# Two state-space layers and a convolution tail on one core: Softplus in one function, sums of two tiles together, a second product tile on GpSimd, and a new slot table

## The chip, the core and the metric

The kernel runs on one core of a Trainium2 chip, in float32 throughout. The metric is the device time of one execution in microseconds (us). The kernel before takes 7343.06 us, the median of three runs (7335.37 to 7346.82). The profiled execution has a span of 7346.1 us.

## What is computed

Four layers follow one another on an input of 8 images, 384 channels, 32 by 32 pixels, so 1024 tokens per image. Layers 0 and 1 each hold a Mamba block (768 inner channels, 16 states per channel), layer 1 also a channel gate and an MLP (384 to 1536 to 384). Layers 2 and 3 are 13 by 13 depthwise convolutions with a 1 by 1 convolution between. The change touches the Mamba blocks, whose core is:

```python
u = silu(conv(x_in) + conv_b)
dt_lo, Bm, Cm = split(u @ x_proj_w.T)                # 24, 16 and 16 columns
delta = softplus(dt_lo @ dt_proj_w.T + dt_proj_b)
h = h * exp(delta * A) + delta * u * Bm              # for every token in turn, 768 channels x 16 states
y = sum over states of h * Cm, + u * D
out = (y * silu(z)) @ out_proj_w.T
```

## The kernel before, in words

**Units, blocks, items.** A unit is one layer, one image and one half of its tokens (512 of 1024), so there are 32 units. A unit has six blocks `d` of 128 channels, and a block has eight items `n`. An item holds 64 of the channels (`h` says which 64) and four of the 16 states (`g` says which four): a tile of 128 partitions by two rows of 512 tokens. That makes 1536 items. Before, `h, g = divmod(n, 4)`: four items of one `h` follow each other, then four of the other.

**What one item costs.** Its steps are on four engines:

- `decay` (L528, ScalarE): two `Exp` activations write the factor of the recurrence into the PSUM tile `h`, of which there are two.
- `inflow` (L535, GpSimd): the product `dbu` of `B` and the repeated `delta * u`; four buffers.
- `scan` (L545 for the first half of an image in one instruction, L549 for the second half in two instructions): VectorE runs the recurrence, then multiplies by `C` into a tile `hc` (L554), of which there are three.
- `keep` (L562, ScalarE, first halves only) stores the last state.
- `fold` (L577, TensorE): two products with 32 output columns each sum the states into a quarter of the PSUM tile `acc` each. With `n == 0` the skip product (L573) opens `acc`, and `y_out` (L580, VectorE) takes it away.

For the items in `AT["pool"]`, before only `n == 1`, the multiplication by `C` is done by GpSimd instead (L564, in place), one slot later.

**The step sizes.** For each block, softplus is made of parts: a product into PSUM (L474), then on ScalarE `Abs`, `Relu` and `Exp` (L479 to L481), an `Identity` and a `Ln` (L486, L487), one more `Identity` (L490), and on GpSimd three tile operations that put the result together (L491, L494, L497). A fourth (L502) multiplies by `u`, and a small one (L504, first halves) separates the rows in the scan. `delta` and its product with `u` go to DRAM (`flat`, L508) and come back repeated over the states (`repeat`, L517): two tiles for each of the two, each filled by four transfers.

**The order of work.** There is no automatic scheduling: every engine's queue is the program order that a slot plan writes out by hand. Slot `K` belongs to item `K`. The main loop emits for each slot: `keep` of item K-1, `decay` of item K+1, `inflow` of item K+2, `scan` of item K, `fold` of item K-1, and then everything that the plan has put in this slot. The plan places the projections of the *next* unit (`x`, `z`, `ranks`), its layer norm, the convolution, the batches of `Silu`, the output product of the *last* unit and the MLP of finished images, all by the slot numbers in the table `AT`. Engines work in order, so a waiting instruction holds up all that its queue has behind it.

**Tables of ScalarE.** `Exp` and `Ln` share a table set. `Silu` and the MLP's `Gelu` are in others. So `table` (L446) does a batch of them and then loads the set with `Exp` again (`exp_ln`, L305). Before, each unit has four batches of `Silu` and each MLP four of `Gelu`.

**The end.** After slot 1536 the rest of the plan runs in slot order without scans: here the output products and the MLPs of the last images. Then come the two depthwise passes (L947) and the pointwise product (L981).

Of the kernel before, what the change touches and what calls it, by code (L numbers as in the profile page):

```python
# [16 lines left out]
P = 128  # L17
# [82 lines left out]
class Unit:  # L100


    def __init__(self, layer, b, half):
        self.layer, self.b, self.half = layer, b, half
        self.cols = slice(half * T, (half + 1) * T)
        self.us, self.zs, self.ps, self.acc = [None] * KD, [None] * KD, {}, {}
        self.dr, self.ur, self.o, self.B, self.C, self.w = {}, {}, {}, {}, {}, {}

# [111 lines left out]
AT = {'in_ahead': 2, 'out_ahead': 2, 'taps_ahead': 3, 'norm': (-5, -2, -1, 0, 1, 2, 3, 3, 4, 5, 7, 12, 12, 12, 12), 'x': (13, 16, 18, 24, 26, 29), 'shift': 1, 'conv': 4, 'u': 5, 'silu': ((31, 3, 0), (34, 6, 1), (40, 6, 4), (58, 6, 6)), 'hid': 2, 'ranks': (33, 34, 35), 'z': (31, 35, 37, 39, 40, 41), 'B': (41, 44, 45, 46), 'C': (41, 42, 46, 48), 'step': (3, 4, 5, 6, 6, 7, 7), 'repeat': (13, 13, 15, 15), 'out': (0, 3, 8), 'out_half': 2, 'out_add': 3, 'out_gate': 0, 'res_ahead': 1, 'heads': 14, 'softmax': (16, 18, 19), 'attend': (19, 22, 25, 23), 'context': 29, 'hidden': (30, 31, 32, 34, 36, 38), 'gates': (42, 40, 46), 'mlp': 22, 'mlp_norm': (-6, 1, 2, 2, 3, 4, 5, 5, 5, 5, 7, 9, 9, 11, 11), 'mlp_plan': ((3, 60, 12, (23, 33, 42, 69)), (2, 44, 8, (22, 30, 38, 42)), (2, 44, 7, (18, 28, 40, 44))), 'fold0': (-18, -10), 'fold0_step': (3, 3), 'shifted': 2, 'flat': (9, 9), 'bc_out': 37, 'store': 2, 'mlp_gap': -2, 'px_ahead': 1, 'pool': (1,), 'prepare': (-40, 4),  # L220
# [3 lines left out]
def layers(tc, k, a, vec, x0, x1, x2, x3, lasting, got):  # L224
# [16 lines left out]
    with ExitStack() as st:  # L241
# [87 lines left out]
        def load_dt(s, d):  # L329
            s.w["dt", d] = work.tile([R + 1, P], F32, tag="w_dt", name="w_dt")  # L330
            nc.sync.dma_start(s.w["dt", d], s.layer.w["dt"][:, d * P : (d + 1) * P])
# [116 lines left out]

        def ranks(s, ds):

            if ds[0] == 0:
                s.xps = mm()
            for d in ds:
                nc.tensor.matmul(s.xps[:NX], s.w["xp"][:, d], s.us[d], start=d == 0, stop=d == KD - 1)
# [9 lines left out]
        def spread(s, key, g):  # L464

            t = work.tile([P, T], F32, tag=key, name=key, bufs={"B": 5, "C": 6}[key])
            at = ("BC".index(key) * NS + 4 * g) * T
            nc.sync.dma_start(t, bass.AP(s.bc.tensor, s.bc.offset + at, [[T, 4], [0, 32], [1, T]]))
            getattr(s, key)[g] = t


        def sp_in(s, d):
            s.sp = mm()
            nc.tensor.matmul(s.sp, s.w.pop(("dt", d)), s.dbc[: R + 1], start=True, stop=True)  # L474

        def sp_exp(s, d):
            s.e = work.tile([P, T], F32, tag="sp_e", name="sp_e", bufs=1)
            s.delta = work.tile([P, T], F32, tag="delta", name="delta", bufs=1)
            nc.scalar.activation(s.e, s.sp, AF.Abs)  # L479
            nc.scalar.activation(s.delta, s.sp, AF.Relu)  # L480
            nc.scalar.activation(s.e, s.e, AF.Exp, scale=-1.0)  # L481

        def sp_ln(s, d):
            s.one = work.tile([P, T], F32, tag="sp_w", name="sp_w", bufs=1)
            s.ln = work.tile([P, T], F32, tag="sp_l", name="sp_l", bufs=1)
            nc.scalar.activation(s.one, s.e, AF.Identity, bias=k["one"])  # L486
            nc.scalar.activation(s.ln, s.e, AF.Ln, bias=k["one"])  # L487

        def sp_one(s, d):
            nc.scalar.activation(s.one, s.one, AF.Identity, bias=k["minus"])  # L490
            nc.gpsimd.tensor_tensor(s.one, s.one, s.e, ALU.subtract)  # L491

        def sp_back(s, d):
            nc.gpsimd.tensor_tensor(s.ln, s.ln, s.one, ALU.subtract)  # L494

        def sp_delta(s, d):
            nc.gpsimd.tensor_tensor(s.delta, s.delta, s.ln, ALU.add)  # L497

        def sp_du(s, d):

            s.du = work.tile([P, T], F32, tag="sp_w", name="sp_w", bufs=1)
            nc.gpsimd.tensor_tensor(s.du, s.delta, s.us[d], ALU.mult)  # L502
            if s.half == 0:
                nc.gpsimd.tensor_tensor(s.delta[:, 0:1], s.delta[:, 0:1], far, ALU.add)  # L504

        def flat(s, d, which):
            got = dram.tile([P, T], F32, tag="dd" if which == "d" else "uu", name="dd" if which == "d" else "uu")
            nc.sync.dma_start(got, s.delta if which == "d" else s.du)  # L508
            (s.dr if which == "d" else s.ur)[d] = got, {}

        def repeat(s, d, which, h):

            dd, got = (s.dr if which == "d" else s.ur)[d]
            got[h] = work.tile([P, 2, T], F32, tag=f"r{which}", name=f"r{which}", bufs=2)
            for q in range(4):
                quarters = bass.AP(dd.tensor, dd.offset + 64 * h * T, [[T, 32], [32 * T, 2], [1, T]])
                nc.sync.dma_start(got[h][32 * q : 32 * q + 32], quarters)  # L517
# [4 lines left out]
        def decay(item):  # L522
            s, d, n = item
            h, g = divmod(n, 4)
            y = ps_h.tile([P, 2, T], F32, tag="h", name="h")
            for q in range(2):
                at = (d * 4 + 2 * h + q) * 4 + g
                nc.scalar.activation(y[:, q], s.dr[d][1][h][:, q], AF.Exp, scale=s.layer.A[:, at : at + 1])  # L528
            ready[item, "h"] = y

        def inflow(item):
            s, d, n = item
            h, g = divmod(n, 4)
            dbu = work.tile([P, 2, T], F32, tag="dbu", name="dbu", bufs=4)
            nc.gpsimd.tensor_tensor(dbu, s.B[g].unsqueeze(1).to_broadcast([P, 2, T]), s.ur[d][1][h], ALU.mult)  # L535
            ready[item, "dbu"] = dbu

        def scan(item):
            s, d, n = item
            h, g = divmod(n, 4)  # L540
            y, dbu = ready.pop((item, "h")), ready.pop((item, "dbu"))
            to = dbu if n in AT["pool"] else y
            if s.half == 0:
                flat_to, flat_y, flat_b = (t.rearrange("p q t -> p (q t)") for t in (to, y, dbu))
                nc.vector.tensor_tensor_scan(flat_to, flat_y, flat_b, 0.0, ALU.mult, ALU.add)  # L545
            else:
                for q in range(2):
                    first = state[:, d, 2 * h + q, g : g + 1]
                    nc.vector.tensor_tensor_scan(to[:, q], y[:, q], dbu[:, q], first, ALU.mult, ALU.add)  # L549
            ready[item, "h"] = to  # L550
# [6 lines left out]
        def keep(item):  # L557
            s, d, n = item
            h, g = divmod(n, 4)
# [3 lines left out]
            if n in AT["pool"]:  # L563
                nc.gpsimd.tensor_tensor(y, y, s.C[g].unsqueeze(1).to_broadcast([P, 2, T]), ALU.mult)  # L564
                ready[item] = y

        def fold(item):

            s, d, n = item
            h, g = divmod(n, 4)  # L570
# [3 lines left out]
            hc = ready.pop(item)  # L574
            for q in range(2):
                r = 2 * h + q
                nc.tensor.matmul(s.acc[d][32 * r : 32 * r + 32], k["fold"], hc[:, q], start=False, stop=g == 3)  # L577
# [62 lines left out]
        def pooled_in(s, c):  # L640
            s.px = work.tile([P, T], F32, tag="px", name="px", bufs=1)
# [117 lines left out]
        for i, s in enumerate(units):  # L759

            lay, at = s.layer, (i - 1) * SLOTS
            norm(s, lay.src[s.b], "xt", at, AT["norm"] if i else (-2 * SLOTS,) + AT["norm"][1:])
# [9 lines left out]
            u0 = z0 = 0  # L772
            for j, (e, u1, z1) in enumerate(AT["silu"]):
# [4 lines left out]
                u0, z0 = u1, z1  # L778
            put(at + AT["ranks"][0] - 6, load_xp, s)
# [12 lines left out]
            for d in range(KD):  # L792
                at = i * SLOTS + (d - 2) * PER
                steps = AT["step"]
                put(at + steps[0] - 5, load_dt, s, d)
                put(at + steps[0], sp_in, s, d)
                put(at + steps[1], sp_exp, s, d, first=True)
                for e, f in zip(steps[2:], (sp_ln, sp_one, sp_back, sp_delta, sp_du)):
                    put(at + e, f, s, d)
                for e, (which, h) in zip(AT["repeat"], (("u", 0), ("d", 0), ("u", 1), ("d", 1))):  # L800
                    put(at + e, repeat, s, d, which, h)
                put(at + AT["flat"][0], flat, s, d, "d")
                put(at + AT["flat"][1], flat, s, d, "u")
# [45 lines left out]
        for b in range(B):  # L849
            for half in range(L // T):  # L850
# [4 lines left out]
                pace_up, down, pace_down, tables = AT["mlp_plan"][max(b - B + 3, 0)]  # L855
# [18 lines left out]
                at += down + KC * pace_down + AT["mlp_gap"]  # L874
# [10 lines left out]
        with tc.manual_schedule(engines={E.Activation, E.DVE, E.Pool, E.PE, E.SP}):  # L885
            exp_ln()
            for K in range(min(plan.slots), n_items + 1):
                if K > 1 and (K - 2) % PER in AT["pool"]:
                    fold(item(K - 2))
                if 0 < K <= n_items:  # L890
                    keep(item(K - 1))
                for ahead, f in ((1, decay), (2, inflow)):
                    for j in range(K, K + ahead) if K == 0 else ():
                        f(item(j))
                    if 0 <= K < n_items - ahead:
                        f(item(K + ahead))
                if 0 <= K < n_items:
                    scan(item(K))
                if K > 0 and (K - 1) % PER not in AT["pool"]:
                    fold(item(K - 1))  # L900
# [262 lines left out]
```

## Time and profile before

| part of the execution | from, to (us) | what runs |
|---|---|---|
| start | 0 to 150 | weights are scaled, first norm and projections |
| scans | 150 to 6360 | 1536 items with all that lies beside them |
| rest of the plan | 6360 to about 6630 | output products and MLPs of the last image |
| convolutions | about 6630 to 7346 | depthwise, pointwise, depthwise |

The first and last numbers of the scans are the start of the first `dbu` (149.8) and the end of the last sum (about 6361). Over the whole span the engines are busy for 6375.0 us (TensorE), 6097.4 (VectorE), 5600.1 (GpSimd) and 4775.5 (ScalarE). In the page, a group of instructions has its number of instructions behind the x, then its busy time and the mean of one, and then the idle time of the engine just before them with what ended it. A product in float32 is two instructions on TensorE, so 5376 instructions of L577 are 2688 products.

### The profile page before, as it was taken

To read this page: it belongs to the slowest core of one execution; us is meant where nothing else is said; L and a number is where in the kernel's file an instruction comes from. 1 tells how busy PE (TensorE), PEld (TensorE's weight loads), DVE (VectorE), ACT (ScalarE), POOL (GpSimd) and SP (SyncE) were. 2 spreads that over 40 slices of the span, in tenths; PEclk is the share of its full clock that TensorE was granted. 3 is DMA by queue.
4 is the path that set the end of the run, shared out by engine and by line. 5 is a ranking of instruction groups with operands and counts; after the bars stand their busy time and mean duration, and the time that the engine had idled before them with its cause. 6 is when DMAs were issued, how large, how long until landed. Compare 5 with 4: busy or idle time off the path is not lost. (4 is left out here: it accounts for less than half of the span.)

```text
span 7346.1 us, 79965 instructions
## 1 busy us (share of the span) xinstructions
PE 6375.0 (87%) x22562; PEld 2193.7 (30%) x22562; DVE 6097.4 (83%) x5167; ACT 4775.5 (65%) x8246; POOL 5600.1 (76%) x3330
## 2 busy tenths in 40 slices
PE   6888888999899999998899989998999989677877
PEld 2222222222222222223222322222222323225556
DVE  3999999898989989988999898989899888607456
ACT  4777676877686767686777768776767676321121
POOL 2989888888888879888888788888888787513123
PEclk7888888999999999999999999999999999899898
DMA  4655555565556555656565655555566656327677
GB/s 127 173 168 151 147 158 146 155 167 164 160 160 167 169 158 153 173 157 172 152 166 161 170 153 156 167 165 160 158 166 169 166 153 160 91 72 196 199 197 178
DMA packets 983807, 1172.05 MB, mean 160 GB/s; under 512 B 314248, under 2 KB 579016, under 8 KB 983368
## 3 DMA queue, kind: packets, MB, share of 16 engines
q1 hardware_dynamic: 844872, 1089.94, 53.9%
q10 hardware_dynamic: 120064, 42.48, 2.2%
q0 software_dynamic: 18432, 34.53, 1.8%
q8 instruction: 184, 3.01, 0.2%
q14 instruction: 255, 2.09, 0.1%
HBM read 911.75 MB, written 204.21 MB: 152 GB/s over the span
## 5 line engine op out<-in xcount | busy, mean ns | idle before, releaser
L535 POOL TENSOR_TENSOR dbu<-B,ru 128x1024 f32<-128x1024 f32 x1536 | 3588.3, 2359 | 286.6 <-DMA ru<-uu 108.9
L528 ACT ACTIVATE h<-rd,A 128x512 f32<-128x512 f32 x3072 | 2121.8, 691 | 752.9 <-DVE hc L554 557.0
L549 DVE TENSOR_TENSOR_SCAN h<-h,state,dbu 128x512 f32<-128x512 f32 x1344 | 1729.7, 1287 | 176.7 <-POOL dbu L535 103.6
L554 DVE TENSOR_TENSOR hc<-h,C 128x1024 f32<-128x1024 f32 x1344 | 1646.2, 1225 | 120.4 <-DMA C<-bc 18.9
L577 PE MATMUL acc<-hc,fold 128*32 128x512 f32 x5376 | 1470.2, 629 | 315.7 <-DVE hc L554 313.2
L545 DVE TENSOR_TENSOR_SCAN h<-h,dbu 128x1024 f32<-128x1024 f32 x672 | 1538.3, 2289 | 192.6 <-ACT h L528 167.9
L405 PE MATMUL mm<-xt,wi 128*128 128x512 f32 x2304 | 1146.1, 634 | 54.8 <-DMA wi<-w_in 21.9
L687 PE MATMUL f<-mx,wi 128*128 128x512 f32 x1152 | 626.9, 639 | 68.3 <-ACT fh L691 46.7
L405 PEld LDWEIGHTS mm<-xt,wi 128*128 128x128 f32 x2304 | 425.2, 198 | 774.5 <-issue 476.6
L933 POOL DMA_DIRECT2D xp<-x x384 | 223.5, 584 | 562.9 <-PE ps L947 303.3
L700 PE MATMUL f<-fh,wo 128*128 128x512 f32 x1152 | 612.8, 628 | 23.2 <-DVE rows_out L706 20.5
L577 PEld LDWEIGHTS acc<-hc,fold 128*32 128x32 f32 x5376 | 214.1, 110 | 1357.0 <-DVE hc L554 739.5
L491 POOL TENSOR_TENSOR sp_w<-sp_w,sp_e 128x512 f32<-128x512 f32 x192 | 244.2, 1272 | 489.5 <-ACT sp_w L490 351.4
L947 PE MATMUL ps<-xp,wt 128*32 128x256 f32 x6144 | 423.1, 423 | 167.4 <-DMA wt<-k_rows 111.6
L596 PE MATMUL mm<-u,wo 128*128 128x512 f32 x1152 | 550.3, 614 | 14.1 <-DMA wo<-in_l_out_dram 13.8
L564 POOL TENSOR_TENSOR dbu<-dbu,C 128x1024 f32<-128x1024 f32 x192 | 452.5, 2357 | 76.3 <-DVE dbu L549 42.1
L952 ACT ACTIVATE o<-ps,b 128x256 f32<-128x256 f32 x192 | 91.2, 475 | 522.5 <-PE ps L947 444.4
L947 PEld LDWEIGHTS ps<-xp,wt 128*32 128x32 f32 x6144 | 352.4, 144 | 238.9 <-issue 176.0
L429 PE MATMUL mm<-xp,taps 128*64 128x512 f32 x1536 | 400.5, 644 | 3.5 <-DVE sq L646 2.0
L687 PEld LDWEIGHTS f<-mx,wi 128*128 128x128 f32 x1152 | 197.2, 193 | 467.7 <-issue 314.6
L940 DVE COPY xp<-xp 32x702 f32<-32x702 f32 x384 | 199.7, 520 | 165.3 <-DMA xp<-x 146.6
L596 PEld LDWEIGHTS mm<-u,wo 128*128 128x128 f32 x1152 | 212.6, 194 | 349.3 <-issue 289.5
(150 smaller groups left out, 7364.9 us busy)
## 6 DMA issues: line engine op xcount, KB each, us to landing
ru<-uu SPq DMA_DIRECT2D x1536, 128.0 KB
rd<-dd SPq DMA_DIRECT2D x1536, 128.0 KB
wi<-w_in SPq DMA_DIRECT2D x384, 192.0 KB
xp<-xp SPq DMA_DIRECT2D x384, 128.5 KB
dd<-delta SPq DMA_DIRECT2D x192, 256.0 KB
uu<-sp_w SPq DMA_DIRECT2D x192, 256.0 KB
wt<-k_rows SPq DMA_DIRECT2D x768, 64.0 KB
wo<-in_l_out_dram SPq DMA_DIRECT2D x96, 384.0 KB
```

The lines of the kernel that those rows point to most:

```text
L405: nc.tensor.matmul(s.ps[m], w[:, c], s.xt[:, c], start=c == 0, stop=c == KC - 1)
L528: nc.scalar.activation(y[:, q], s.dr[d][1][h][:, q], AF.Exp, scale=s.layer.A[:, at : at + 1])
L535: nc.gpsimd.tensor_tensor(dbu, s.B[g].unsqueeze(1).to_broadcast([P, 2, T]), s.ur[d][1][h], ALU.mult)
L545: nc.vector.tensor_tensor_scan(flat_to, flat_y, flat_b, 0.0, ALU.mult, ALU.add)
L549: nc.vector.tensor_tensor_scan(to[:, q], y[:, q], dbu[:, q], first, ALU.mult, ALU.add)
L554: nc.vector.tensor_tensor(hc, to, s.C[g].unsqueeze(1).to_broadcast([P, 2, T]), ALU.mult)
L564: nc.gpsimd.tensor_tensor(y, y, s.C[g].unsqueeze(1).to_broadcast([P, 2, T]), ALU.mult)
L577: nc.tensor.matmul(s.acc[d][32 * r : 32 * r + 32], k["fold"], hc[:, q], start=False, stop=g == 3)
L596: nc.tensor.matmul(s.ps[m], w[:, d], s.us[d], start=d == 0, stop=d == KD - 1)
L687: nc.tensor.matmul(s.ps[m], s.w["in", m][:, c], s.xt[:, c], start=c == 0, stop=c == KC - 1)
L700: nc.tensor.matmul(s.down, s.w["out", 2 * m + f // KD][:, f % KD], s.hs[f], start=f == 0, stop=f == KF - 1)
L947: nc.tensor.matmul(ps[HW * q : HW * (q + 1), : B * HW], wt[:, q, :, j], x[:, q, :, 4 * j : 4 * j + HW], start=j == 0, stop=j == KP - 1,)
```

## The change

The change does five things.

1. `Softplus` is one activation from PSUM (`step_size`). It has a table set of its own, so it runs in three batches of two blocks per unit (`soft`: slots 37, 45 and 62, counted from one unit ahead), each followed by the load of the `Exp` set. GpSimd keeps the product with `u` and the small separating operation.
2. Items are counted `g, h = divmod(n, 2)`, so two neighbours are the two halves of the channels with the same states. `fold` takes two tiles at once, at even slots, and issues four products to the four quarters of `acc` one after the other.
3. `AT["pool"]` is `(0, 6)`: GpSimd multiplies two of eight items by `C`, into an `hc` tile and no longer in place.
4. Buffers: the repeated tiles have three buffers each instead of two, `B` and `C` four instead of five and six; `delta` and its product share four; the tiles of the old softplus go.
5. The slot table is new in most entries, with the layer norm of the first unit placed on its own (`norm0`), and the MLP of the last image but one paced like the earlier ones.

`inject`, a way to do the second halves in one scan, is in the code and switched off (`'inject': 0`).

```diff
-'repeat': (13, 13, 15, 15) ... 'pool': (1,) ... 'step': (3, 4, 5, 6, 6, 7, 7) ... 'flat': (9, 9)
-'silu': ((31, 3, 0), (34, 6, 1), (40, 6, 4), (58, 6, 6)) ... 'in_ahead': 2
-'mlp_plan': ((3, 60, 12, (23, 33, 42, 69)), (2, 44, 8, (22, 30, 38, 42)), (2, 44, 7, (18, 28, 40, 44)))
+'repeat': (9, 12, 12, 13) ... 'pool': (0, 6) ... 'soft': ((37, 2), (45, 4), (62, 6)), 'du': 1, 'flat_u': 2
+'silu': ((28, 3, 0), (34, 6, 0), (40, 6, 4), (57, 6, 6)) ... 'in_ahead': 3
+'mlp_plan': ((3, 60, 12, (21, 33, 44, 69), -2), (1, 48, 7, ...), (2, 46, 6, (18, 30, 36, 46), -2), (1, 36, 4, (22, 30, 36, 36), -2))
...
+        def step_sizes(s, ds):
+            for d in ds:
+                step_size(s, d)
+            exp_ln()
...
-        def sp_exp(s, d):
-            nc.scalar.activation(s.e, s.sp, AF.Abs)
-            nc.scalar.activation(s.delta, s.sp, AF.Relu)
-            nc.scalar.activation(s.e, s.e, AF.Exp, scale=-1.0)
...
-        def sp_one(s, d):
-            nc.scalar.activation(s.one, s.one, AF.Identity, bias=k["minus"])
-            nc.gpsimd.tensor_tensor(s.one, s.one, s.e, ALU.subtract)
...
+        def step_size(s, d):
+            ps = mm()
+            nc.tensor.matmul(ps, s.w.pop(("dt", d)), s.dbc[: R + 1], start=True, stop=True)
+            s.delta[d] = work.tile([P, T], F32, tag="delta", name="delta", bufs=4)
+            nc.scalar.activation(s.delta[d], ps, AF.Softplus)
...
-            got[h] = work.tile([P, 2, T], F32, tag=f"r{which}", name=f"r{which}", bufs=2)
+            got[h] = work.tile([P, 2, T], F32, tag=f"r{which}", name=f"r{which}", bufs=3)
...
-            h, g = divmod(n, 4)
+            g, h = divmod(n, 2)
...
-                nc.gpsimd.tensor_tensor(y, y, s.C[g].unsqueeze(1).to_broadcast([P, 2, T]), ALU.mult)
-                ready[item] = y
+                hc = work.tile([P, 2, T], F32, tag="hc", name="hc", bufs=3)
+                nc.gpsimd.tensor_tensor(hc, y, s.C[g].unsqueeze(1).to_broadcast([P, 2, T]), ALU.mult)
+                ready[item] = hc
...
-            hc = ready.pop(item)
-            for q in range(2):
-                r = 2 * h + q
-                nc.tensor.matmul(s.acc[d][32 * r : 32 * r + 32], k["fold"], hc[:, q], start=False, stop=g == 3)
+            tiles = [ready.pop(item) for item in pair]
+            for r in range(4):
+                nc.tensor.matmul(
+                    s.acc[d][32 * r : 32 * r + 32], k["fold"], tiles[r // 2][:, r % 2], start=False, stop=n == PER - 2
+                )
...
-                if K > 1 and (K - 2) % PER in AT["pool"]:
-                    fold(item(K - 2))
+                if K > 0 and K % 2 == 0:
+                    fold((item(K - 2), item(K - 1)))
```

## The prediction

> **What bounds the kernel now.** The 1536 items between 150 and 6361 us set the time; all else is about 1135 us. I read first the busy times by stage, for the stretch in which items run undisturbed, and the same for L535 alone to count the items.
>
> ```profile
> 200.00:6200.00 6000.00, 5385.47 (x15121) 1628.85 (x15118) 5421.73 (x4063) 4393.05 (x7578) 5155.66 (x2811) 0.96 0.58 162
> 200.00:6200.00 6000.00, 3459.90 (x1481) 0.96 0.58 162
> ```
>
> The columns of the first line are TensorE, its weight loads, VectorE, ScalarE and GpSimd. VectorE and TensorE are both busy for 90% of the stretch, GpSimd for 86%, ScalarE for 73%. The second line counts 1481 items (185 blocks), so an item takes 4.05 us. No engine is full; four queues that work in order wait for each other. VectorE carries the recurrence and is idle for 578 of 6000 us. Next, its waits in this stretch, longest in total first:
>
> ```profile
> DVE h L545 <- ACT h L528: 163.6, 91, 7.3
> DVE h L549 <- POOL dbu L535: 103.1, 52, 4.0
> DVE u L580 <- PE acc L577: 44.3, 25, 4.9
> DVE h L549 <- ACT h L528: 35.6, 31, 2.8
> DVE dbu L545 <- ACT h L528: 18.7, 18, 2.3
> DVE h L545 <- POOL dbu L535: 18.6, 11, 2.1
> DVE hc L554 <- DMA C<-bc: 18.4, 13, 2.6
> ```
>
> So about 218 us of `decay` on ScalarE, 122 of GpSimd, 74 of TensorE (44 here and smaller rows), 18 of transfers; 146 are gaps too small to name. ScalarE is only 73% busy, so why is it late? The timeline near 4010 us shows a case:
>
> ```profile
> 4010.40 0.60 ACT L479 ACTIVATE sp_e<-mm 128x512 f32<-128x512 f32 x1 [3.23 <-PE mm L474]
> 4010.89 0.59 ACT L480 ACTIVATE delta<-mm 128x512 f32<-128x512 f32 x1
> 4011.37 0.63 ACT L481 ACTIVATE sp_e<-sp_e 128x512 f32<-128x512 f32 x1
> 4012.66 1.42 ACT L528 ACTIVATE h<-rd,A 128x512 f32<-128x512 f32 x2
> 4014.18 2.30 DVE L545 TENSOR_TENSOR_SCAN h<-h,dbu 128x1024 f32<-128x1024 f32 x1 [1.29 <-ACT h L528]
> ```
>
> TensorE is behind, the first step of softplus waits 3.23 us for its product, `decay` stands behind it, and VectorE loses 1.29 us. TensorE at 90% reaches VectorE through ScalarE's queue. Last, the groups that the change touches:
>
> ```profile
> L554 DVE TENSOR_TENSOR hc<-h,C 128x1024 f32<-128x1024 f32 x1344 | 1646.2, 1225 | 120.4 <-DMA C<-bc 18.9 <-DVE h L549 1.8 <-PE acc L577 0.5
> L564 POOL TENSOR_TENSOR dbu<-dbu,C 128x1024 f32<-128x1024 f32 x192 | 452.5, 2357 | 76.3 <-DVE dbu L549 42.1 <-ACT state L562 32.9 <-DMA wo<-in_l_out_dram 0.9
> L494 POOL TENSOR_TENSOR sp_l<-sp_l,sp_w 128x512 f32<-128x512 f32 x192 | 243.7, 1269 | 15.1
> L486 ACT ACTIVATE sp_w<-sp_e,one 128x512 f32<-128x512 f32 x192 | 136.0, 708 | 0.1
> L305 ACT ACT_TABLE_LOAD x193 | 247.6, 1283 | 4.2 <-PEq L1151 0.7
> 3002.38 1.05 PE L577 MATMUL acc<-hc,fold 128*32 128x512 f32 x4
> 3003.36 1.12 PE L700 MATMUL f<-fh,wo 128*128 128x512 f32 x2
> 6731.06 8.94 PE L947 MATMUL ps<-xp,wt 128*32 128x256 f32 x128 [3.37 <-DVE xp L940]
> ```
>
> The last three are from the timeline of TensorE.
>
> **What the skill says.** The Trainium skill, "TensorEngine Tiling (Array Packing)", section "Key Properties": tiles of the array work in parallel, and a change of the tiling mode drains the array. The trace agrees: the convolutions, four products of 32 columns side by side, take 8.94 us for 128 instructions of 256 columns, 70 ns each; and a pair of L700 takes 1.06 us in front of L577 (3001.32 to 3002.38), against 0.90 in a row (12 in 5.42). The Trainium skill, "ScalarE: Activation LUTs", section "What ACT_TABLE_LOAD costs": a load is 1283 ns, with a drain of some 1380 ns beside it, and every function costs the same per element. The trace has 1283 ns exactly and shows no drain (a load at 4021.15 is followed by its activation at 4022.44). The Trainium skill, "GPSIMD Engine Reference", section "1. Specifications": GpSimd shares its SBUF interfaces with VectorE and the two contend where VectorE has two SBUF inputs. Here one input of the scan and of `hc` is PSUM, and L554 takes 1223 to 1227 ns whatever GpSimd does; so I add nothing for contention.
>
> **The change, part by part, for these 185 blocks.**
>
> *Second tile to GpSimd.* VectorE loses 185 x 1.225 = 227 us, GpSimd gains 185 x 2.357 = 436. The new wait: the product waits for its scan and has the next `inflow` behind it. After the end of that scan GpSimd needs 2 x 2.36 = 4.7 us; VectorE wants that `dbu` two slots later, some 7 us on. That leaves 2.4 us for other GpSimd work in the slot.
>
> *Softplus.* ScalarE loses six activations per block, 0.586 + 0.589 + 0.630 + 0.708 + 0.708 + 0.711 = 3.93 us, so 727. One Softplus comes back, not in this trace: between 0.59 (`Relu` from PSUM) and 0.69 (`Exp` with a scale from SBUF); I take 0.59, 109 us. Two loads per batch of two blocks: 93 x 2 x 1.283 = 239. ScalarE: -379. GpSimd loses three operations, 185 x 3.81 = 705. With the tile product it nets -269.
>
> A batch is 2 x 1.283 + 2 x 0.59 = 3.75 us in a row. `decay` of the next slot stands behind it, and VectorE after that. After its own `decay` (1.42) ScalarE has about 2.2 us free before the next can begin, and that can be 2.1 late before VectorE notices. So a lone batch fits in 4.3 us and costs nothing; with a wait for its product, as above, it costs 1 to 3. I take 0.7 us on average, 65 us, and 0 to 2 as bounds. The two products with `u` come in one slot, 2 x 1.27 + 2 x 0.19 = 2.9 us, against the 2.4 above: three times per unit perhaps 0.5 to 1 us.
>
> *Sums of two tiles.* Before, two groups of 0.98 us per pair of items and two changes of mode; after, eight instructions of 2 x 70 ns = 1.12 us and one change. 0.84 + about 0.2 = 1.0 us, I take 0.9: 740 pairs, 666 us of TensorE, and a sum waits only at every second slot. Nothing of it is on VectorE's path directly; it shortens ScalarE's waits for products.
>
> *Buffers and slots.* The third repeated tile lets the first half of the next block load early. The second half can only start when item 6 has been read, and is read again by item 1 of the next block: three slots, about 9 us with one short slot, for a transfer that took 7.3 us at 3022 (issue 3022.18, its reader starts at 3029.51). Mostly hidden. Fewer buffers of `B` and `C` cost nothing: in the new order a state group is done with after two items, so `B` is loaded five slots ahead of its first use and `C` four, behind the items between.
>
> *The end.* In the changed program's order of instructions 22 products of the first and 36 of the second MLP matrix are left after the last sum, before the two last MLPs; before it was 25 of the second. 33 more at 0.45 x 2 = 0.9 us, 30 us; some norm work now overlaps, so +25. The start (+-10) and the convolutions keep their times.
>
> **The sum.** Busy in 6000 us would be: VectorE 5195, GpSimd 4887, TensorE 4720, ScalarE 4014. VectorE is then the clear bound. Its idle time: ScalarE 218 to 165 (TensorE's share halved, plus 65), GpSimd 122 to 145, TensorE 74 to 45, transfers 18 to 25, small gaps 146 to 130: 510. 5195 + 510 = 5705, or 0.951 of 6000. 0.951 x 6211 = 5906, 305 saved; 7343 - 305 + 25 = 7063, rounded 7060.
>
> **The rivals.**
> - *The queues come apart* (25%): with 12% less work TensorE hardly delays anyone, and idle time falls to 330. For it: VectorE would be 6% above GpSimd and 10% above TensorE instead of level with it. Against: table batches remain. 5525 / 6000 x 6211 = 5719; 7343 - 492 + 20 = 6871.
> - *Batches take the place of the old waits* (8%): 2 us for each of 93 on top of 578 is 764. 5959 / 6000 x 6211 = 6168; 7343 - 43 + 25 = 7325.
> - *Second halves arrive late* (10%, slower): 7.3 us was one transfer's time, and a queue with others in it can make it 10 or more; 2.5 us per block is 463 us on top of 510. 6168 / 6000 x 6211 = 6385; 7343 + 174 + 25 = 7542. Against: transfers are busy 58%, and waits for `rd` hardly reach VectorE now.
>
> The forecast keeps 57%. A range of 6800 to 7300 leaves out most of the last two and the far end of the first. Faster 0.86, same 0.03, slower 0.11.
>
> **What would show it.** Right: VectorE near 91% in the scans and GpSimd next; L554's successor 1152 times; Softplus near 0.6 us, 96 more loads on each side of it; TensorE's sums near 0.9 ms for all 3072 products; waits of ScalarE for TensorE halved. Wrong: waits of `decay` for `rd` above 100 us (late halves), of the scan for `decay` above 300 (batches), of the scan for `dbu` above 250 (GpSimd as bound), or an end more than 60 us longer.

## The result

The changed kernel takes 7130.71 us (median of 4 runs, 7121.62 to 7134.86) against 7339.22 us before: a ratio of 0.9717, with a 95% interval of 0.9697 to 0.9736. So it is 208 us faster. The forecast was 283 us faster (7060 us), with a range that holds the measured time.

All experiments below were timed beside runs of the kernel before on the same chip. They are compared by their ratios to it. One per cent of the ratio is 73 us. Unless it is said otherwise, each edit is to the changed kernel.

### The profile page after: what moved, and what is told of

It is laid out like the page before. It is cut to its first block, busy times and chain, and to the rows that moved or that the text cites. A ratio compares the mean times of both kernels' runs of the same rounds, so it can differ in the third digit from the quotient of the medians.

```text
span 7119.8 us, 78637 instructions
## 1 busy us (share of the span) xinstructions
PE 5950.9 (84%) x22562; PEld 2191.2 (31%) x22562; DVE 5844.4 (82%) x4975; ACT 4472.8 (63%) x7478; POOL 5321.3 (75%) x2946
## 4 chain that ended last, share of the span: by engine, by line
PE 27%; DVE 23%; ACT 16%; issue 10%; DMA 8%; POOL 3%; SPq 1%; DVEq 0%; POOLq 0%; ACTq 0%
DVE h L544 9%; PE mm L406 7%; DVE h L547 5%; ACT h L516 5%; PE acc L574 3%; PE f L686 3%; PE f L699 3%; DVE hc L552 3%; ACT L447 2%; PE ps L982 2%; ACT L306 2%; POOL dbu L523 2%; DVE dbu L547 2%; DVE dbu L544 1%; PE mm L480 1%
## 5 line engine op out<-in xcount | busy, mean ns | idle before, releaser
L544 DVE TENSOR_TENSOR_SCAN h<-h,state,dbu 128x512 f32<-128x512 f32 x1152 | 1482.0, 1286 | 92.2 <-POOL delta L491 36.0
L552 DVE TENSOR_TENSOR hc<-h,C 128x1024 f32<-128x1024 f32 x1152 | 1410.8, 1225 | 114.7 <-PE acc L574 23.6
L547 DVE TENSOR_TENSOR_SCAN h<-h,dbu 128x1024 f32<-128x1024 f32 x576 | 1318.2, 2289 | 151.0 <-ACT h L516 119.3
L574 PE MATMUL acc<-hc,fold 128*32 128x512 f32 x6144 | 1147.7, 661 | 268.3 <-DVE hc L552 216.4
L563 POOL TENSOR_TENSOR hc<-dbu,C 128x1024 f32<-128x1024 f32 x384 | 903.9, 2354 | 526.6 <-DVE dbu L544 230.7
L406 PE MATMUL mm<-xt,wi 128*128 128x512 f32 x2304 | 1195.0, 659 | 97.8 <-ACT delta L482 26.2
L406 PEld LDWEIGHTS mm<-xt,wi 128*128 128x128 f32 x2304 | 449.4, 207 | 821.3 <-issue 569.8
L574 PEld LDWEIGHTS acc<-hc,fold 128*32 128x32 f32 x6144 | 164.0, 112 | 1096.2 <-DVE hc L552 494.4
L544 DVE TENSOR_TENSOR_SCAN dbu<-h,state,dbu 128x512 f32<-128x512 f32 x384 | 470.5, 1267 | 24.9 <-ACT h L516 18.4
L547 DVE TENSOR_TENSOR_SCAN dbu<-h,dbu 128x1024 f32<-128x1024 f32 x192 | 438.0, 2281 | 20.3 <-ACT h L516 17.8
L486 POOL TENSOR_TENSOR delta<-delta,u 128x512 f32<-128x512 f32 x192 | 241.4, 1268 | 226.8 <-ACT delta L482 224.3
```

The source lines that it names most:

```text
L406: nc.tensor.matmul(s.ps[m], w[:, c], s.xt[:, c], start=c == 0, stop=c == KC - 1)
L547: nc.vector.tensor_tensor_scan(flat_to, flat_y, flat_b, first, ALU.mult, ALU.add)
L552: nc.vector.tensor_tensor(hc, to, s.C[g].unsqueeze(1).to_broadcast([P, 2, T]), ALU.mult)
L563: nc.gpsimd.tensor_tensor(hc, y, s.C[g].unsqueeze(1).to_broadcast([P, 2, T]), ALU.mult)
```

## The profile after

First the busy times of one long stretch, and the count of `dbu` products there. The columns are those of the first fence of the prediction, but this stretch is 5800 us long.

```profile
200.00:6000.00 5800.00, 4988.93 (x15154) 1629.76 (x15156) 5214.08 (x3907) 4117.35 (x6855) 4908.66 (x2445) 0.93 0.62 168
200.00:6000.00 5800.00, 3482.81 (x1491) 0.93 0.62 168
```

VectorE is busy for 5214.08 / 1491 = 3.497 us per item. Before it was 5421.73 / 1481 = 3.661, and the prediction's sum gives 5195 / 1481 = 3.508. But VectorE is idle for 586 / 1491 = 0.393 us per item, and it was 578 / 1481 = 0.390 before. The prediction had 510 / 1481 = 0.344. This difference of 0.049 us, over 1536 items, is 75 us more than forecast. The work is 0.011 us per item, 17 us in all, less than forecast. Together that is 58 us, and the profiled execution (7121.6 us) lies 62 us above the forecast (the median lies 71 above). So the gain in the scans is work taken off VectorE; the fall in its idle time, which the forecast had too, did not come. The other parts came as forecast: the last sum starts at 6111.1 us and 1009 us follow it (986 before; +23 measured, +25 forecast), and the first scan starts at 144.2 us instead of 153.2.

Next, VectorE's waits in the stretch from 200 to 5800 us, which is the one used for all comparisons below:

```profile
DVE u L579 <- PE acc L574: 160.7, 79, 5.7
DVE h L547 <- ACT h L516: 113.3, 75, 3.1
DVE h L544 <- POOL delta L491: 36.0, 30, 3.4
DVE h L544 <- ACT h L516: 35.3, 46, 2.4
DVE hc L552 <- PE acc L574: 23.3, 28, 2.5
```

The first line is new in its size: the product L579 that takes a block's finished sum away (L580 before) waited 32 us in this stretch of the kernel before, and now waits 161 us for TensorE. The sums over the whole list, with those of the kernel before in brackets, are: TensorE 201 us (53), ScalarE 203 (204), GpSimd 53 (113), transfers 0 (18). So what VectorE no longer waits for GpSimd and for transfers, it waits for TensorE, and more. Its waits for ScalarE are what they were.

The groups of the changed parts, from the page and its longer list:

```profile
L552 DVE TENSOR_TENSOR hc<-h,C 128x1024 f32<-128x1024 f32 x1152 | 1410.8, 1225 | 114.7 <-PE acc L574 23.6
L563 POOL TENSOR_TENSOR hc<-dbu,C 128x1024 f32<-128x1024 f32 x384 | 903.9, 2354 | 526.6 <-DVE dbu L544 230.7
L574 PE MATMUL acc<-hc,fold 128*32 128x512 f32 x6144 | 1147.7, 661 | 268.3 <-DVE hc L552 216.4
L482 ACT ACTIVATE delta<-mm 128x512 f32<-128x512 f32 x192 | 105.8, 595 | 12.4 <-PE mm L480 11.3
L482 ACT ACT_TABLE_LOAD x96 | 123.2, 1283 | 21.7 <-PE mm L480 19.0 <-DMA skip<-in_l_skip_dram 0.9 <-issue 0.7
```

The unit costs are the predicted ones: 1225 and 2354 ns for the product with `C`, 595 ns for Softplus (0.59 was taken), 1283 ns for a load. Each batch needs one for Softplus (the 96 of L482) and one back (the page has 289 loads at L306 and had 193 before). GpSimd waits 231 us for VectorE in front of L563: it is not the bound. (Over the stretch from 200 to 5800 us it is busy for 85%, just behind TensorE with 86%; VectorE has 90%.) TensorE's sums are busy for 1148 us (1470.2 + 205.5 = 1676 before), not for the 860 of 768 groups of 1.12 us. The timeline of TensorE shows both kinds of group:

```profile
3004.95 1.05 PE L574 MATMUL acc<-hc,fold 128*32 128x512 f32 x4
3007.83 1.05 PE L574 MATMUL acc<-hc,fold 128*32 128x512 f32 x4 [1.83 <-DVE hc L552]
3029.19 1.07 PE L574 MATMUL acc<-hc,fold 128*32 128x512 f32 x8
```

Eight instructions side by side take 1.07 us, as long as four. But where TensorE starts on the first tile and then waits for the second, the pair takes two groups of 1.05 us again. Counted over the whole trace, 619 of the 768 pairs run as eight in a row, 441 of these in less than 1.25 us, and 149 are split. In the kernel before, neighbours went to the same two quarters of `acc`, and eight in a row, of which it has 201, took 1.91 us in the median.

How L579 comes to wait, in the timeline a little later:

```profile
3014.55 1.75 DVE L369 TENSOR_TENSOR mx<-mx,mm 128x1536 f32<-128x1536 f32 x1
3016.22 2.45 DVE L544 TENSOR_TENSOR_SCAN dbu<-h,state,dbu 128x512 f32<-128x512 f32 x2
3016.39 0.63 ACT L375 ACTIVATE sq<-mx 128x512 f32<-128x512 f32 x1 [4.20 <-DVE mx L369]
3017.08 2.08 PE L376 MATMUL mm<-sq,avg 128*128 128x512 f32 x2 [3.55 <-ACT sq L375]
3019.08 1.94 PE L574 MATMUL acc<-hc,fold 128*32 128x512 f32 x8
3021.09 0.69 DVE L579 TENSOR_TENSOR u<-acc,zs 128x512 f32<-128x512 f32 x1 [2.42 <-PE acc L574]
```

Item 0 of the next block is now a short slot: its scan (2.45 us) ends at 3018.67 and no `hc` product follows on VectorE. L579 is next in line. TensorE meanwhile stood for 3.55 us before a product of a layer norm, and the block's last sums stood behind it. This case has a second part. The view by stretches gives the granted clock of TensorE as 1.00 from 3008 to 3016 us, and as half of it just after the long wait:

```profile
3016.50:3022.50 6.00, 5.42 (x12) 1.54 (x13) 3.58 (x4) 3.81 (x7) 4.47 (x3) 0.50 0.11 30
```

There the two instructions of L376 take 2.08 us and the eight of the sums 1.94, where the same groups take 1.02 (at 3024.63) and 1.07 (at 3029.19) at the full clock. So nearly 2 us of this delay are the slow clock, where L579 waits 2.42 us. It is not the rule: of the 161 us that L579 waits, 21 fall into stretches of half clock.

## The experiments

Two theories of these 75 us of idle time were set against each other. Theory A: L579's wait for TensorE, new in its size, is the loss, and what removes it gains its time. Theory B: ScalarE hands `decay` over late, with the table loads of the batches among its work, and L579's wait only stands in the place of waits for ScalarE; removing it uncovers those.

### Late L579

```diff
+            if n == 1 and late:            # in scan, between the recurrence and the product with C
+                y_out(*late.pop())
...
-                put(at + 24, y_out, s, d, first=True)
+                put(at + 24, late.append, (s, d), first=True)
```

The very last block keeps its old place.

> The changed kernel with one move: the product that takes a finished block's sum away (L579) stands behind the scan of item 1 of the next block instead of behind the scan of item 0. Theory A (the sum is now on VectorE's path: item 0 is short since its second product went to GpSimd, so VectorE reaches L579 before TensorE has done the last four products): the wait of L579 falls from 170 us to under 40 and the time falls by 110 to 190 us, to about 6980. Theory B (VectorE's idle time only moves: it was 9.6% before the change and 10.1% after): the wait of L579 falls as well, but others take its place, and the time stays within 50 us of 7130.

Measured: 7089.45 us, ratio 0.9675 (0.9659 to 0.9691), 31 us better than the changed kernel. The waits from 200 to 5800 us:

```profile
DVE h L547 <- ACT h L516: 175.7, 111, 3.0
DVE h L544 <- ACT h L516: 55.7, 69, 2.5
```

The wait of L579 is gone from the list, and the waits for `decay` have gone from 149 us in these rows to 231. VectorE is idle for 564 us there, with 1448 items: 0.389 us per item, which is 5 us over 1536 items less than the 0.392 of the changed kernel. Most of the 31 us come from its busy time, 3.478 us per item instead of 3.494; over the whole span it is 5817.2 us instead of 5844.4, so 27 us less for the same instructions. The timeline of VectorE shows where:

```profile
2011.21 2.30 DVE L547 TENSOR_TENSOR_SCAN h<-h,dbu 128x1024 f32<-128x1024 f32 x1 [1.72 <-ACT h L516]
2013.42 0.67 DVE L581 TENSOR_TENSOR u<-acc,zs 128x512 f32<-128x512 f32 x1
2014.01 1.21 DVE L554 TENSOR_TENSOR hc<-h,C 128x1024 f32<-128x1024 f32 x1
```

The moved product (L581 here) starts 0.09 us before the scan ends, and the product with `C` 0.08 us before the moved one ends. In the changed kernel, where the product with `C` needs the scan just before it, it starts 0.03 us after the scan's end (2025.99 after 2023.66 + 2.30). By this account the gain is mostly this overlap, and taking away the wait of 161 us gave some 5 us of idle time. Theory B stands in its core: removing one wait only uncovered another, here that for ScalarE.

### Items 2 and 6 on GpSimd

```diff
-'pool': (0, 6)
+'pool': (2, 6)
```

> The changed kernel with items 2 and 6 on GpSimd instead of 0 and 6. The number of products on each engine is the same; item 0 is long again, so VectorE has 1.2 us more work ahead of L579. Theory A: the wait of L579 falls from 170 us to about 60, and the time by 60 to 110 us. Theory B: the time stays within 50 us of 7130.

Measured: 7165.25 us, ratio 0.9777 (0.9761 to 0.9794), 44 us slower than with (0, 6). L579's wait falls to 51 us, so the short item 0 does make it. But the waits for `decay` rise:

```profile
DVE h L547 <- ACT h L516: 200.6, 123, 3.5
DVE u L579 <- PE acc L574: 51.0, 53, 4.0
```

Theory A foresaw 60 to 110 us gained, and Theory B a time within 50 us of 7130, which is what came. The edit also gives GpSimd its tile in another slot, so the loss of 44 us is not the price of one wait; but a wait 110 us shorter did not make the kernel faster, and Theory A is wrong about what it is worth.

### Sums item by item

```diff
-            tiles = [ready.pop(item) for item in pair]
-            for r in range(4):
+            hc, h = ready.pop(pair[0]), n % 2
+            for q in range(2):
+                r = 2 * h + q
...
```

> The changed kernel with the sums issued item by item, two products each, as before the change; all else as changed. The prediction's step (four side by side spare TensorE some 0.9 us per pair, 690 us in all, and this reaches VectorE only through ScalarE's waits): TensorE's busy time rises by 500 to 690 us and the time by 60 to 150 us. Theory A adds that the last sum of a block comes in two smaller pieces but behind a busier TensorE: the wait of L579 stays at 120 us or more. Rival (the pairs gave nothing): the time stays within 30 us. If the lower granted clock (0.92 against 0.94) comes from the pairs, the clock goes back to 0.94.

Measured: 7195.38 us, ratio 0.982 (0.9798 to 0.9841), 76 us slower than in pairs. TensorE's sums take 1379.6 us instead of 1147.7. So the pairs spare 232 us of TensorE's time, and not the 500 to 690 expected: without them the sums of 378 of the 768 pairs still ran as eight in a row, where TensorE was behind, and 294 of these in less than 1.25 us. The time moved as the prediction's step asked (60 to 150 us). ScalarE waits 499 us for TensorE here from 200 to 5800 us and 398 with pairs, and VectorE 251 us for ScalarE (203) and 104 for GpSimd (53). L579's wait (L578 here) is 135 us. The granted clock was 0.924 (0.919 with pairs), so it does not go back to the 0.94 of before.

### Relu in place of Softplus

```diff
-            nc.scalar.activation(s.delta[d], ps, AF.Softplus)
+            nc.scalar.activation(s.delta[d], ps, AF.Relu)
...
-            exp_ln()                       # in step_sizes
```

> The changed kernel with Relu in place of Softplus and without the loads of the Exp set behind these batches: same operands, no table loads there (leaves softplus out of the computation). The prediction took 0.7 us for each of 93 batches, 65 us, with bounds of 0 and 186: the time falls by about 65 us. If batches are what keeps VectorE idle (the second rival of the prediction): it falls by 150 us or more, and ScalarE's share of VectorE's waits (209 us) halves. Theory A by itself expects 20 to 80 us.

Measured: 6985.78 us, ratio 0.9536 (0.952 to 0.9552), 133 us faster than the changed kernel. VectorE's idle time is 453 us for 1473 items, 0.308 us per item instead of 0.392; 0.084 x 1536 = 129 us, so all of the gain is idle time. This version leaves softplus out of the computation.

```profile
DVE u L578 <- PE acc L573: 141.1, 81, 3.7
DVE h L546 <- ACT h L515: 83.6, 65, 2.8
```

The loads of 96 batches cost 133 us, 1.4 us per batch; the prediction took 0.7, with 2 as its upper bound. The gain lies between the two expectations (65, or 150 and more): VectorE's waits for ScalarE fall from 203 to 144 us, not to half. Part of it goes by GpSimd: the wait for L491, which stands behind the product with `u` that waits for Softplus, was 36 us and is 12 in this run.

### Only item 6 on GpSimd

```diff
-'pool': (0, 6)
+'pool': (6,)
```

> The changed kernel with only item 6 on GpSimd: the second product is back on VectorE. VectorE gains 192 x 1.225 = 235 us of work. Theory B (VectorE's idle time per item, 0.39 us before and after the change, does not depend on which wait is named): the time rises by about 235 us. Theory A (item 0's short slot is what makes L579 wait, 170 us): L579's wait falls below 60 and the time rises by 70 to 130 us only.

Measured: 7246.35 us, ratio 0.9872 (0.9858 to 0.9887), 114 us slower than with two. Both numbers of the expectation are met on Theory A's side: L579's wait is 56 us. VectorE has 3.649 us of work per item here (5162.90 / 1415) and only 0.309 us of idle time. Over the whole span VectorE's work is 6086.1 us here and 5844.4 in the changed kernel: the second tile took 242 us off it and gave half of that back as idle time. Theory B's sharper form, an idle time per item that never depends on the work, is wrong. That does not bring Theory A back: with more work VectorE comes later to everything it waits for, so this run does not price L579's wait alone, as the first one does.

### The kernel before with two items on GpSimd

```diff
-'pool': (1,)
+'pool': (1, 6)
```

> The kernel before with items 1 and 6 on GpSimd, and nothing else. VectorE loses 235 us, GpSimd gains 453 on top of its 86%: 93% busy at the old pace, more than VectorE's 86%. The prediction's arithmetic: GpSimd becomes the bound, and the time rises by 50 to 250 us. Rival (VectorE's work alone sets the time): it falls by some 150 us or more.

Measured: 7636.86 us, ratio 1.0412 (1.0395 to 1.043), 302 us slower than before, where 50 to 250 were expected. From 200 to 5800 us, the busy times and the longest waits of VectorE:

```profile
200.00:5800.00 5600.00, 4817.93 (x13389) 1472.90 (x13389) 4674.22 (x3458) 3913.16 (x6764) 4996.77 (x2682) 0.94 0.56 153
...
DVE u L580 <- PE acc L577: 302.1, 131, 5.1
DVE h L549 <- POOL dbu L535: 141.0, 86, 4.7
DVE h L545 <- POOL dbu L535: 109.7, 74, 2.6
```

GpSimd is the busiest engine (89%), and VectorE waits 251 us for its `dbu`. L580's 302 us are GpSimd's too in good part: the sums of the tiles that it multiplies (L577 with `dbu`) have TensorE wait 475 us for them, 19 before. Taking VectorE's work away makes this kernel slower. Only items 1 and 6 were tried, and here GpSimd multiplies in place, in a `dbu` buffer that is then free later; how much of the 302 us is the place and how much GpSimd's load was not separated.

### The kernel before with Softplus as one function

```diff
...
-            nc.scalar.activation(s.e, s.sp, AF.Abs)
-            nc.scalar.activation(s.delta, s.sp, AF.Relu)
-            nc.scalar.activation(s.e, s.e, AF.Exp, scale=-1.0)
+            nc.scalar.activation(s.delta, s.sp, AF.Softplus)
+            exp_ln()
...
-                for e, f in zip(steps[2:], (sp_ln, sp_one, sp_back, sp_delta, sp_du)):
+                for e, f in zip(steps[6:], (sp_du,)):
```

> The kernel before with Softplus as one function, one block at a time (six batches per unit, so 384 table loads and not 192), and without its six activations and three GpSimd operations; nothing else. VectorE's work is unchanged. ScalarE is 0.8 us per block lighter, GpSimd 3.8. By the cost of the batches in the changed kernel (133 us for 96) 192 batches would cost some 200 to 270 us against the old chain's waits. If the old chain cost VectorE little: the time rises by 100 to 250 us. If the old chain was as bad (ScalarE's 218 us of VectorE's waits were mostly its doing): it stays within 60 us.

Measured: 7416.28 us, ratio 1.0107 (1.0092 to 1.0122), 78 us slower than before. This lies between the two cases, and below what the loads alone were expected to cost: so the old chain was not free either. GpSimd is lighter (4138 us busy in 5600, 74%), and VectorE's waits for its `dbu` go from 111 us to 3. In their place its waits for ScalarE grow from 204 us to 346. So this run has one gain and one larger loss in it. It has six batches of one block per unit, twice the loads of the changed kernel, and does not show what three batches would have done here.

### No tables at all

This edit is to the kernel with Relu; the functions of the other batches, Silu and Gelu, become copies, so they too are left out of the computation.

```diff
-                nc.scalar.activation(t, t, f)
-            exp_ln()
+                nc.scalar.activation(t, t, AF.Identity)
```

> The run with Relu in place of Softplus, and in addition Identity in place of every batch of Silu and Gelu in the two layers, with no table loads at all there (leaves these functions out of the computation). ScalarE loses 384 more loads of 1.283 us, 493 us. If VectorE's idle time is made by ScalarE's batches in front of the decays: its idle time per item falls from 0.31 to about 0.2 us and the time by another 100 to 170 us, to about 6850. If TensorE's lateness makes it: by less than 50 us.

Measured: 6911.04 us, ratio 0.9414 (0.9397 to 0.943), 90 us faster than with Relu alone, a little under the 100 to 170 of the first expectation and well over the 50 of the second. Idle time per item is 398 / 1490 = 0.267 us. The waits for `decay` in front of VectorE are almost gone (42 us in the longest row), and L579's has stayed:

```profile
DVE u L577 <- PE acc L572: 143.9, 92, 5.6
...
DVE h L545 <- ACT h L514: 42.1, 51, 1.5
```

The gain per load falls from 133 / 192 = 0.7 us to 90 / 384 = 0.23: the batches of Silu and Gelu stand where they hurt less, or what they cost is covered by L579's wait.

### Ln(1 + Exp(x))

```diff
-            nc.scalar.activation(s.delta[d], ps, AF.Softplus)
+            nc.scalar.activation(s.delta[d], ps, AF.Exp)
+            nc.scalar.activation(s.delta[d], s.delta[d], AF.Ln, bias=k["one"])
...
-            exp_ln()                       # in step_sizes
```

> The changed kernel with Softplus as Ln(1 + Exp(x)), both in the set that is loaded anyway: 192 loads go, 192 activations of about 0.7 us come. ScalarE loses 246 - 134 = 112 us net. If the cost of the batches (133 us with all of it gone) is the loads in front of the decays: the time falls by 70 to 110 us, to about 7040. If it is the mere row of work in one slot: two blocks take 2 x 1.3 = 2.6 us in a row instead of 3.8, and it falls by 30 to 60.

Measured: 7009.57 us, ratio 0.9555 (0.9539 to 0.9571), 119 us faster than the changed kernel and a little above the upper end of what was expected. `Exp` and `Ln` share the set that is loaded, so no load is needed. `Ln` takes 722 ns per block, 139 us of ScalarE, and yet the time is only 14 us behind that of the run with Relu. So 246 us of loads cost 133 us, and 139 us of activations in the same places about 14. Whether that is the loads as such, or that a row of 2.6 us still fits in front of a decay and one of 3.8 us does not, the runs do not separate.

### Ln(1 + Exp(x)) and late L579

The edits of the first experiment and of the one above, together.

> The same with the late L579 of the first experiment. Alone that move took away 161 us of wait and gave 31 us, since ScalarE's decays came late instead. Theory B (what was hidden behind L579 is ScalarE's lateness): with ScalarE relieved the move gives more than 31 us here, 50 to 90. Rival (the 31 us are all there is to have): it gives 31 us again, and the two add up to about 7010.

Measured: 6962.86 us, ratio 0.9495 (0.9466 to 0.9525), 44 us better than the last. The interval is about 22 us on each side, so this run alone does not say that the late L579 is worth more here than its 31 us. The point estimate is under Theory B's 50 to 90. VectorE's busy time over the whole span falls by 31 us (5844.0 to 5813.1), as in the first experiment, and its longest wait for `decay` grows from 112 to 169 us. So even with ScalarE relieved of the loads, the wait that was removed is mostly replaced. The version is the fastest of all that leave nothing out: 5% below the kernel before, 2.3% below the changed one.

### A lighter TensorE

```diff
-            nc.tensor.matmul(s.ps[m], s.w["in", m][:, c], s.xt[:, c], start=c == 0, stop=c == KC - 1)
+            if c == KC - 1:
+                nc.tensor.matmul(s.ps[m], s.w["in", m][:, c], s.xt[:, c], start=True, stop=True)
```

It leaves out two thirds of the first matrix product of the MLP.

> The changed kernel with one of three products for each part of the MLP's hidden layer (leaves two thirds of that matrix product out of the computation): TensorE loses 384 products of 0.9 us, some 340 us, of which about 57 lie behind the last sum. The prediction's step (a lighter TensorE frees VectorE through ScalarE's queue and through the sums): the part with the scans gets shorter by 60 to 120 us, and L579's wait falls by half. If TensorE's lateness is not what holds VectorE: the part with the scans stays within 25 us.

Measured: 7059.75 us, ratio 0.9629 (0.9613 to 0.9645), 65 us faster than the changed kernel. The last sum starts at 6069.7 us instead of 6111.1, so 41 us of it are in the scans, the rest behind them. That is between the two expectations. L579's wait is 141 us (161 before), not half. So less work on TensorE alone does not bring the sums in time. That fits waits for a predecessor in its queue, as in the timeline at 3017.08, but it is not a clean test of the amount of work. TensorE's busy time per item falls only from 4814 / 1441 = 3.341 us to 4685 / 1449 = 3.234, which is 165 us over 1536 items where some 280 were expected beside the scans, and the granted clock falls to 0.895.

### Second tile first

This edit is to the version with `Ln(1 + Exp(x))` and late L579.

```diff
-            for r in range(4):
+            for r in (2, 3, 0, 1):
```

> The kernel of the last experiment but one (Ln(1 + Exp(x)), late L579), with the four products of a pair in another order: the two of the second tile first. In the trace of the changed kernel many pairs start on the first tile and then wait for the second (two groups of 4 instructions of 1.05 us each, as at 3004.95 and 3007.83); with the second first, all eight run side by side in 1.06 us. TensorE's time for the sums falls from 1121 us towards 814 (768 x 1.06). By the light-MLP run (281 us of TensorE less in the window gave about 40 us in the scans) the time falls by 20 to 45 us, to about 6930. Rival (TensorE waits for the second tile anyway, so its saved time is idle time): the sums get shorter, and the time stays within 10 us.

Measured: 7005.67 us, ratio 0.9551 (0.9537 to 0.9565), 41 us *slower* than without, which neither expectation had. The sums got shorter as expected, and what was spared became waiting. The group of sums in the kernel without the edit, and then with it:

```profile
L576 PE MATMUL acc<-hc,fold 128*32 128x512 f32 x6144 | 1121.4, 659 | 238.2 <-DVE hc L554 204.3 <-POOL hc L565 32.1
```

```profile
L576 PE MATMUL acc<-hc,fold 128*32 128x512 f32 x6144 | 938.6, 674 | 389.1 <-DVE hc L554 386.7 <-POOL hc L565 1.0
```

183 us less busy, 151 us more idle before it. The granted clock is 0.919 in the profiled run, against 0.934. From 200 to 5800 us TensorE has half the clock for 808 us with the edit and for 614 without. That the lower clock is what turns the balance from zero to 41 us fits, but was not tested by itself.

## Why the prediction was right, and where it was off

The direction was right, the range held the time, and the gain came out at three quarters of the forecast. Of the mechanism, one half was right: work went off VectorE, and GpSimd had been made free for it. The other half, less idle time on VectorE because TensorE is lighter, did not come.

- **VectorE's work.** The step "VectorE loses 185 x 1.225 = 227 us" is right: 3.497 us per item against 3.508 forecast. The kernel before with two tiles on GpSimd shows that this step does not stand alone: there it costs 302 us. The prediction's sum has GpSimd's three operations out and one tile in, and GpSimd is indeed no bound in the changed kernel.
- **TensorE on VectorE's path.** The step "Nothing of it is on VectorE's path directly" failed, and with it the term "TensorE 74 to 45". L579 reads every block's sum and stands behind one scan, which has no product behind it now that item 0 is GpSimd's: 161 us. Items 2 and 6 in place of 0 and 6 bring it down to 51. What this wait cost is another matter: without it the idle time was only 5 us less. The 0.9 us per pair was too much as well: 1676 - 1148 = 528 us of busy time over 768 pairs is 0.69, since 149 pairs run in two groups and 178 of the other 619 take 1.25 us or more, 84 of them under the half clock.
- **TensorE through ScalarE's queue.** The step "it shortens ScalarE's waits for products" is right in its direction: 398 us with pairs, 499 without. But its size was not: these waits were 429 us before, and the prediction's sign of being right, "waits of ScalarE for TensorE halved", did not come. That "GpSimd next" in busy time did not either; TensorE is.
- **The batches.** The term of 0.7 us per batch, 65 us, was mis-sized: the loads of 96 batches measured 133 us, 1.4 each, inside the stated bounds. The 68 us more are about as much as the 75 us of idle time that the forecast did not have; since such terms do not simply add, this is a fit in size and no proof. With TensorE's share hardly shorter and the batches dearer, VectorE's waits for ScalarE did not fall from 218 us to 165: they are 203 us in 5600, and were 204.
- **GpSimd.** The term "122 to 145" was too high: 53 us in 5600, of which 36 are the row behind L491. Most of that row goes with the loads of the batches (12 us in the run with Relu), so the two products with `u` in one slot, which the term was raised for, cost little.
- **Sum of the terms.** For as many items as the prediction's stretch has (1481), the waits of the changed kernel are ScalarE 209 us (forecast 165), GpSimd 55 (145), TensorE 206 (45), transfers 0 (25), small gaps 111 (130): 581 in all, forecast 510. Two terms were too low by 205 us together and three too high by 134. That the sum is only 71 us off is luck in part. The late L579 shows why adding such terms is unsafe: 161 us of wait could be removed for 5 us of idle time.
- **The rivals.** Late second halves did not come: ScalarE waited for `rd` for 20 us (45 before) in 5600. The batches did cost, 1.4 us each where that rival needed 2, but the waits of the old chain went at the same time. The queues did not come apart.
- **The end** cost 23 us, 25 forecast.

What stays open: how much of the rest of the idle time is the alternation of ScalarE and VectorE over two PSUM tiles. A third one was not tried. Nor were the old softplus in the changed kernel, or the old slot table with the other parts new, so the runs do not say what Softplus and the slot table by themselves brought.

## What to carry to other kernels

Moving work between engines has to be read as a whole: here the second tile product made the kernel before 302 us slower by itself, and Softplus, one block at a time, 78 us; together, with new slots, they are part of a kernel 208 us faster. Where queues in order wait for each other, the listed wait of the bound engine is not the gain (here 161 us of wait were worth 5 us of idle time): look for what comes next behind it. Taking out the table loads of the Softplus batches gained 119 to 133 us, more than moving L579 did. Before a function in another table set is brought in, it is worth writing it with functions of the set that is loaded: `Ln(1 + Exp(x))` with an activation more was 119 us faster than Softplus with its loads.

## What was not expected of the hardware

The clock that TensorE is granted was mostly lower where TensorE had less to do. From 200 to 5800 us it was busy for 90% in the kernel before, 86% in the changed one and 84% with the light MLP; the clock of this stretch is 0.96, 0.93 and 0.91. With Relu (87%) it is 0.94, with `Ln(1 + Exp(x))` and late L579 (87%) 0.95, and with the second tile first (85%) 0.93. The order is not strict: without pairs TensorE was busy for 88%, and the clock was 0.93. The same projections (L405, then L406) took 634 ns and then 659 ns per instruction. So a part of what is spared on TensorE is taken back by a slower clock.

The traces say more than these means. The clock has two values in them, full and half, and the stretch above has half of it for 492 us in the kernel before, for 808 in the changed one and for 1031 with the light MLP. In the changed kernel TensorE stands still for 3 us or longer 43 times; 37 times the clock is at half at some moment of the 3.4 us after the wait (the stretches of one clock in the traces are multiples of that, but for the last). After 77 of the 106 waits of 2 to 3 us it is, and after 56 of the 186 of 1 to 2 us. In the kernel before these are 25 of 26, 58 of 75 and 27 of 124. So it goes with single long waits more than with the mean share, and the changed kernel has more of them. No edit set the length of such a wait by itself, so this is a reading of the traces and not a test.
